# Four changes of order in a four-layer graph network kernel: the gather of layer 0, the first y2T, the aggregate and the last output tile

## The chip, the core and the metric

The kernel runs on one core of one Trainium2 chip. The metric is the device time of one execution in microseconds (us). The core has five engines that run side by side, each taking its own instructions in order: PE (TensorE, matrix products and transposes; PEld is its loading of weights), DVE (VectorE), ACT (ScalarE), POOL (GpSimd) and SP (SyncE, which here only issues transfers, DMAs). They wait for each other through semaphores. SBUF is the working memory of 128 partitions, PSUM the smaller memory that PE writes to.

## The reference

Node features x (8 graphs of 2048 nodes with 64 features) go through four layers with one adjacency matrix A (2048 x 2048, most entries zero, each row of equal entries that sum to 1). Each layer adds its result to x and normalises over the features:

```python
x = _layernorm(x + _L0_gnn_ref(x, adj, embedding, weight, bias))   # layer 0
x = _layernorm(x + _L1_gnn_ref(x, H, adj, 64, W, W_ind, ...))      # layer 1
x = _layernorm(x + _L2_gnn_ref(x, adj, weight_self, weight_neighbor, bias))
x = _layernorm(x + _L3_gnn_ref(x, adj, W))
```

Layer 0 takes x, A x and 2 A (A x) - x, and applies to each node its own 3 x 64 x 64 weights, which are a sum over 16 matrices weighted by the node's embedding:

```python
w = jnp.einsum('nd,dkio->nkio', embedding, weight)
x_g = jnp.einsum('knm,bmc->bnkc', A_stack, x)
out = jnp.einsum('bnki,nkio->bno', x_g, w)
```

Layer 1 is a hypergraph layer. Of it only the beginning matters here: every hyperedge gets a weighted mean of its members' features, with softmax weights,

```python
h = x @ W
alpha = jax.nn.softmax(jnp.where(H.T > 0, s[:, None, :], NEG), axis=-1)
agg = jnp.einsum('ben,bnf->bef', alpha, h)
```

and everything after (gates, edge scores, the weights of the edges at a node) needs agg. Layers 2 and 3 are a product with A (layer 3: A plus the identity, scaled by degrees), a 64 x 64 projection, the sum and the normalisation.

## The kernel before

The nodes lie in 16 tiles of 128 (NT = 16, index j); a tile of features is 128 x 512 (8 graphs by 64 features). A is used as a mask of zeros and ones times one number per row, and float32 products with the mask are made in two fast passes, with the high part (hi) and the rest (lo) of the other factor.

**Before layer 0**, `first_product` (from L453) makes A x for all tiles, and the product with the mask again for tile 0 (L600).

**Layer 0** is the loop at L1786. For each tile it makes eight groups, `weigh` (L1447): a group is 12 products on PE (pp, L1457) into one of two PSUM buffers (tag "pp"), and four multiply-adds on DVE (L1468) that add them, weighted by the embedding, to the tile's result r. A group can begin on PE when DVE is through with the group two before it. The order of all other steps is written out by hand between the groups: everything in a `program_order()` block keeps, on PE, DVE, ACT and POOL, the order in which the code stands. SP is not among these engines; transfers on it are put in order by the compiler's scheduler.

After group 4 of tile j comes `visit(j)` (L1712). It works for several tiles at once: `gather(j - 2)` (L1658) adds tile j-2's weighted features to the sums of all hyperedges, aggp, with two products on PE, whose inputs are hs_hi and hs_lo; `normed(j - 1, ...)` (L1485) finishes tile j-1's normalisation and writes x1; `compare(j + 1, ...)` (L1364) checks on DVE that a half tile of A is what mask times row value gives; `product(j + 1)` (L1409) makes the second product, 32 matmuls, y2p; `mask(j + 2, ...)` (L1318) makes and stores the masks of tile j+2; `counted` and `to_features` (L1433, L1549) make small products and transposes of x1; `second_term(j + 1)` (L1424) transposes y2 on PE and subtracts x on DVE, which gives y2T, the third input of `weigh` in the next tile. Between groups, POOL makes the scaled masks ms that `compare` reads (`scaled`, L1322), sums (`summed`, L1331) and the start of the next r (`begin_sum`, L1377); after group 7, `weighted` (L1640) makes hs_hi and hs_lo.

Buffers are taken by tag: tiles of one tag and pool share its `bufs` buffers in turn, and the compiler makes the first write of a new tile wait for all uses of the one whose buffer it gets. Two lines of that matter:

```python
x1s[j] = tile("y1" if j == NT - 2 else "x1", f"x1_{j}", bufs=1)                 # L1496
lo = tile("y1" if j == NT - 2 else "x1", f"hs_lo_{j}", bufs=1)                  # L1653
```

At the start of layer 0 (L1774 to L1785) the comparisons of tile 0 run in quarters (`compare_first`, L1356), with `second_term(0)` after them. At its end `last_tile` (L1739) does the normalisation and projection of tile 15 in halves, with products of layer 1 between them (`early`), the last gathers, and rden, the reciprocal of the sum of softmax weights.

**Layer 1** begins with the list `head` (L704), a string of steps that `perform` goes through: c.agg makes agg = aggp x rden on DVE (L733), c.hexp and c.he an ELU of it on ACT and DVE, c.trhe transposes it on PE (L168), and so on to the edge scores; 0.i and 1.i are products of the industry term that fill PE in between.

**Layers 2 and 3** (L1989 on) are not in a `program_order()` block: the scheduler orders their instructions. Layer 3's loop (L2045) makes, for each tile, 32 matmuls of 512 columns (L1918), and the normalisation on DVE and ACT (L2051, L137 to L156), and sends the output from ACT's queue (L2056).

Of the kernel before, what the change touches and what calls it, by code (L numbers as in the profile page):

```python
# [19 lines left out]
P = 128  # L20
# [38 lines left out]
def r_(ap):  # L59
    return ap.bitcast(F32R)  # L60
# [3 lines left out]
def kernel(  # L64
# [58 lines left out]
    def b_view(t2):  # L123
        return t2.rearrange("p (b c) -> p b c", b=B)

    def bcast(small):
        return small.unsqueeze(2).to_broadcast([P, B, C])
# [484 lines left out]
    def layer1(  # L612
# [86 lines left out]
        def column_view(src):  # L699
# [2 lines left out]
            )[:, :, :, :, 0]  # L702

        head = (  # L704
            "1.mask 2.mask 3.mask 4.mask c.agg 0.i c.hexp c.he 0.ind c.trhe c.agg1 c.heT "
            "c.fche c.sums c.the c.nagg 1.i c.sep 1.i c.serow c.sert 1.i c.ese c.eexp c.ese2 "
            "c.dnp c.ext 1.i c.rec c.hgr c.dnp2 1.i c.late "
        )
        with tc.tile_pool(name="fa", bufs=2) as fa:
# [8 lines left out]
                for n, k in (("ftr", 1), ("fmm", 1))  # L718
            )
            with program_order():  # L720
                c = {}
                low = slice(64, P)
                sums = fa.tile([P, 2, B], F32, tag="sums", name="sums", bufs=1)
                late = own.tile([P, NT - NE, 2, B], F32, tag="b0_11", name="rest_sums")
# [1 line left out]
                def parts(dst, full):  # L726

                    nc.vector.tensor_copy(r_(dst), full)
                    nc.vector.tensor_tensor(r_(dst[low]), full[low], dst[low], ALU.subtract)

                def aggregate():
                    c["agg"] = agg = fa.tile([P, BC], F32, tag="hs", name="agg", bufs=3)
                    nc.vector.tensor_tensor(b_view(agg), b_view(aggp), bcast(rden), ALU.mult)  # L733

                def exp_edges():
                    c["he"] = fa.tile([P, BC], F32, tag="xT", name="he")
# [94 lines left out]
                def other_weights():  # L831
# [1 line left out]
                    weight_sums(c["dn2"], NE, NT)  # L833

                perform(head, dict(
                    agg=aggregate, hexp=exp_edges, he=elu_edges, trhe=turn_edges, heT=turned_edges,
                    fche=fc_edges, the=tanh_edges, sep=edge_scores, serow=score_rows, sert=turn_rows,
                    agg1=lambda: parts(agg1, c["agg"]), sums=sum_edges, nagg=negated, ese=capped,
                    eexp=exp_scores, ese2=split_scores, dnp=first_weights, ext=extension,
# [439 lines left out]
    def layer0(  # L1279
# [38 lines left out]
        def mask(j, h):  # L1318
            if (j, h) not in msk:
                msk[j, h] = mask_half(mskp, raws[j][h], j, h)  # L1320
# [382 lines left out]
        def when(j, f, *args):  # L1703
            if 0 <= j < NT:
                f(j, *args)
# [5 lines left out]
        load_x(1)  # L1711
        def visit(j):  # L1712

            when(j - 2, gather)
            if j < NT - 1:
                when(j - 1, normed, 1)
            when(j + 1, compare, 0)
            if j < NT - 1:
                when(j - 1, normed, 2)
            when(j + 1, first_terms)  # L1720
            if j + 1 < NT:
                for _ in product(j + 1):
                    pass
            when(j + 2, mask, 0)
            when(j + 2, mask, 1)
            when(j + 1, compare, 1)
            counted(j + 1, j - 2)
            when(j - 1, to_features)
            if j == NT - 2:
                for t in range(len(kept_i)):  # L1730
                    for y, kept_part in zip((y_hi, y_lo), kept_i[t]):
                        nc.sync.dma_start(y[:, t, :], kept_part)
            when(j + 1, second_term)
            if j == 2:
                nc.vector.tensor_copy(rden, dens[j - 2])
            elif j > 2:
                nc.vector.tensor_tensor(rden, rden, dens[j - 2], ALU.add)

        def last_tile():  # L1739

            last = NT - 1
            early[0](6)
            half_features(0)
            gather(last - 1)
            denp = ps_p.tile([P, 2, 2, 4 * C], F32, tag="pp", name="denp")[:, 0, 0, 0:B]
            nc.tensor.matmul(denp, mds[last - 1], es[:, last - 1, :], start=True, stop=False)
            projected(last, 0)
            half_normed(1, 0)
            half_normed(1, 1)
            copied(last, 0, "sc")  # L1750
            weights_of(last, slice(0, 4))
            copied(last, 0, "h")
            copied(last, 0, "hi")
            half_normed(1, 2)
            half_weighted(0)
            copied(last, 0, "lo")
            early[0](3)
            half_features(1)
            early[0](1)
            projected(last, 1)  # L1760
            copied(last, 1, "sc")
            weights_of(last, slice(4, 8))
            half_weighted(1)
            early[0](1)
            half_gather(0)
            nc.tensor.matmul(denp, mds[last], es[:, last, :], start=False, stop=True)
            half_gather(1)
            nc.vector.tensor_tensor(rden, rden, denp, ALU.add)
            nc.vector.tensor_scalar(rden, rden, TINY, None, op0=ALU.max)
            nc.vector.reciprocal(rden, rden)  # L1770
            for what in ("h", "hi", "lo"):
                copied(last, 1, what)

        with program_order():  # L1774
            begin_sum(0)
            load_xs(1)
            mask(1, 0)
            quarters = [scaled_first(h) for h in range(2)]
            compare_first(0, quarters[0])
            mask(1, 1)  # L1780
            compare_first(1, quarters[1])
            for h in range(2):
                summed(0, h)
            second_term(0)
            scaled(1, 0)  # L1785
            for j in range(NT):  # L1786
                when(j + 2, load_adj)
                when(j + 2, load_x)
                for g in range(8):
                    weigh(j, g)  # L1790
                    if g == 0:
                        if j == 0:
                            load_weights()
                        elif j == 2:
                            late_weights()
                        if j == NT - 1:
                            centred(j - 1, 0)
                            centred(j - 1, 1)
                    elif g == 1:
                        if j < NT - 1:  # L1800
                            when(j - 1, centred, 0)
                        if j:
                            when(j + 1, scaled, 1)
                            when(j + 1, first_sum)
                    elif g == 2 and j == NT - 1:
                        normed(j - 1, 1)
                    elif g == 2 and j == 0:
                        counted(0, -1)
                        scaled(1, 1)
                    elif g == 2:  # L1810
                        centred(j - 1, 1)
                    elif g == 3 and j == NT - 1:
                        normed(j - 1, 2)
                    elif g == 3 and j:
                        next(flags, None)
                    elif g == 4:
                        visit(j)
                        if j == NT - 1:
                            spread()
                    elif g == 5:  # L1820
                        when(j + 2, scaled, 0)
                        when(j + 1, begin_sum)
                        when(j + 2, load_xs)
                        when(j - 1, project, 0)
                        if j == NT - 1:
                            half_normed(0, 0)
                            early.extend(industry_early())
                    elif g == 6:
                        if j == NT - 1:
                            half_normed(0, 1)  # L1830
                            project(j - 1, 1)
                            weights_of(j - 1)
                            weighted(j - 1)
                    elif g == 7 and j < NT - 1:
                        if j == 0:
                            score_weights(box[:, 0:2 * C].rearrange("p (i c) -> p i c", i=2))
                        when(j - 1, project, 1)
                        when(j - 1, weights_of)
                        when(j - 1, weighted)
                    elif g == 7:  # L1840
                        half_normed(0, 2)
            last_tile()
            early.pop(0)


    def short_program(top):
# [142 lines left out]
        with tc.tile_pool(name="mj2", bufs=3) as mjp, tc.tile_pool(  # L1989
# [40 lines left out]
            for j in range(NT):  # L2030
# [11 lines left out]
                if j:  # L2042
                    projected(j - 1)
            projected(NT - 1)
            for j in range(NT):  # L2045
                a = mask_tile(mjp, j, "l3")
                acc = ps_acc.tile([P, BC], F32, tag="acc", name=f"a3_{j}")
                for mt in range(NT):
                    times_mask(acc, a, v_hi, v_lo, mt)
                r = l2p.tile([P, BC], F32, tag="r", name=f"r3_{j}")  # L2050
                nc.vector.scalar_tensor_tensor(  # L2051
                    r, acc, cols_of["sdinv"][:, j:j + 1], x2[:, j, :], op0=ALU.mult, op1=ALU.add
                )
                o = l2p.tile([P, BC], F32, tag="o", name=f"o_{j}")
                layernorm(ln, r, o, f"l3_{j}")
                nc.scalar.dma_start(out[j * P:(j + 1) * P, :], o)  # L2056
# [608 lines left out]
```

## Time and profile before

| | us |
|---|---|
| median of 3 runs | 1230.51 |
| lowest and highest | 1228.17, 1231.52 |
| the profiled execution | 1229.4 |
| its span, first to last instruction | 1227.7 |
| mean granted clock of PE | 0.995 of full speed |

By stage, from the stage view of the trace (busy us of each engine):

| stretch, us | what | PE | DVE | ACT | POOL |
|---|---|---|---|---|---|
| 140 to 165 | start of layer 0 | 21.73 | 18.58 | 1.43 | 22.69 |
| 165 to 650 | layer 0 | 480.28 | 397.83 | 119.20 | 238.34 |
| 650 to 662 | its last tile | 11.91 | 8.88 | 4.61 | 4.90 |
| 662 to 680 | head of layer 1 | 15.66 | 8.91 | 4.56 | 0.07 |
| 680 to 965 | layer 1 | 269.75 | 251.81 | 196.37 | 218.34 |
| 965 to 1227 | layers 2 and 3 | 252.72 | 149.59 | 40.60 | 14.80 |

A line of a timeline reads: start in us, duration in us, engine, line of the code, operation, what is written <- what is read, shapes, count (neighbouring equal instructions are merged and counted; the duration is then that of all), and in brackets how long the engine sat idle before it and whom it waited for. Ends of matmuls are modelled.

### The profile page before, as it was taken

The numbers are of one execution on the slowest core, as the hardware profiler recorded it, in microseconds if no ns is written. First come the engines' busy times: TensorE is split into PE (matmuls) and PEld (weight loads), VectorE is DVE, ScalarE is ACT, GpSimd is POOL, SyncE is SP. The second block draws the span as 40 slices with busy tenths as digits, with TensorE's granted clock in tenths as the row PEclk, the third lists the DMA queues.
The fourth block names the chain that finished last, engine by engine and source line by source line (L and its number), as shares of the span: only waits on it lengthen the run. The fifth ranks groups of instructions, "written<-read, shape, count | busy, mean of one in ns | idle before, by whom it ended". The sixth has DMA issues, their size and how long they took to land.

```text
span 1227.7 us, 19772 instructions
## 1 busy us (share of the span) xinstructions
PE 1187.7 (97%) x7470; PEld 942.0 (77%) x7470; DVE 911.2 (74%) x1671; ACT 388.8 (32%) x1019; POOL 512.4 (42%) x429
## 2 busy tenths in 40 slices
PE   9999899999999999999999999999999999999996
PEld 7777788888888888888886655555557788888885
DVE  4555678888888888888876899988996766665454
ACT  3100102222222222222223667676676411111111
POOL 2000472555555555555511788888881700000000
PEclk9999999999999999999998999999999999999998
DMA  8977943333333333332384113122320333334541
GB/s 282 251 230 222 189 131 104 109 105 113 109 103 107 114 115 114 106 99 99 106 309 147 43 61 110 62 103 104 95 69 2 138 132 109 118 123 163 180 172 71
DMA packets 101848, 157.10 MB, mean 128 GB/s; under 512 B 13041, under 2 KB 64369, under 8 KB 96113
## 3 DMA queue, kind: packets, MB, share of 16 engines
q1 hardware_dynamic: 96944, 151.38, 38.4%
q10 hardware_dynamic: 4368, 4.33, 1.0%
q8 instruction: 61, 1.00, 0.4%
q0 software_dynamic: 432, 0.05, 0.1%
q14 instruction: 43, 0.34, 0.1%
HBM read 117.97 MB, written 37.76 MB: 127 GB/s over the span
## 4 chain that ended last, share of the span: by engine, by line
PE 73%; DVE 13%; DMA 4%; issue 3%; ACT 3%; POOL 2%; SPq 0%; DVEq 0%; ACTq 0%; POOLq 0%
PE pp L1457 26%; PE a L1918 19%; PE y2p L1414 9%; PE y1p L569 5%; PE ind L1918 3%; DMA xraw<-in_xn 2%; DVE d L947 2%; DVE ez L966 1%; DVE gp L944 1%; PE u L1146 1%; DMA adj<-in_at 1%; PE yp L2017 1%; PE try L168 1%; DVE r L1086 1%; PE hp L1582 1%
## 5 line engine op out<-in xcount | busy, mean ns | idle before, releaser
L1468 DVE SCALAR_TENSOR_TENSOR r<-pp,emb_sb,r 128x256 f32<-128x256 f32 x512 | 247.4, 483 | 78.1 <-PE pp L1457 63.9
L1457 PE MATMUL pp<-w_sb,xT 64*128 64x256 f32 x1024 | 155.4, 380 | 0.6 <-DVE r L1468 0.6
L1457 PE MATMUL pp<-w_sb,y2T 64*128 64x256 f32 x1024 | 153.5, 376 | 2.4 <-DVE y2T L1430 2.4
L1457 PE MATMUL pp<-w_sb,y1T 64*128 64x256 f32 x1024 | 153.3, 376 | 0.0
L1326 POOL TENSOR_TENSOR ms<-msk,srow 128x1024 f32<-128x1024 f32 x30 | 76.5, 2552 | 93.8 <-DVE msk L449 93.8
L1457 PEld LDWEIGHTS pp<-w_sb,y2T 64*128 64x128 f32 x1024 | 99.3, 187 | 14.0 <-DVE y2T L1430 2.8
L1457 PEld LDWEIGHTS pp<-w_sb,y1T 64*128 64x128 f32 x1024 | 99.4, 187 | 11.2
L1457 PEld LDWEIGHTS pp<-w_sb,xT 64*128 64x128 f32 x1024 | 95.1, 187 | 12.9 <-issue 2.8
L569 PE MATMUL y1p<-x_hi,m 128*128 128x512 f32 x256 | 103.0, 402 | 1.1 <-DVE y_lo L584 1.1
L569 PE MATMUL y1p<-x_lo,m 128*128 128x512 f32 x256 | 100.5, 393 | 0.0
L1918 PE MATMUL a<-v_hi,mj_l 128*128 128x512 f32 x256 | 100.1, 392 | 0.0
L1918 PE MATMUL a<-v_lo,mj_l 128*128 128x512 f32 x256 | 100.0, 391 | 0.0
L1918 PE MATMUL a<-y_lo,mj_l 128*128 128x512 f32 x240 | 95.1, 396 | 0.0
L1918 PE MATMUL a<-y_hi,mj_l 128*128 128x512 f32 x240 | 94.9, 396 | 0.0
L1414 PE MATMUL y2p<-y_hi,msk 128*128 128x512 f32 x240 | 94.7, 395 | 0.0
L1414 PE MATMUL y2p<-y_lo,msk 128*128 128x512 f32 x240 | 93.5, 390 | 0.0
L1918 PE MATMUL ind<-y_hi,mj_l 128*128 128x512 f32 x208 | 91.2, 438 | 0.1
L1918 PE MATMUL ind<-y_lo,mj_l 128*128 128x512 f32 x208 | 81.9, 394 | 0.0
L971 POOL TENSOR_TENSOR ez<-ez,coef 128x1024 f32<-128x1024 f32 x32 | 65.2, 2039 | 12.8 <-DVE ez L966 12.7
L1366 DVE SCALAR_TENSOR_TENSOR ms<-ms,adj 128x1024 f32<-128x1024 f32 x30 | 67.3, 2242 | 0.0
L1649 POOL TENSOR_TENSOR hs<-h,es 128x512 f32<-128x512 f32 x15 | 15.6, 1042 | 116.1 <-ACT hgr L1621 116.1
L925 POOL TENSOR_TENSOR d<-h,sig 128x1024 f32<-128x1024 f32 (+1 forms) x32 | 50.1, 1569 | 32.6 <-ACT sig L903 18.3
(335 smaller groups left out, 2448.8 us busy)
## 6 DMA issues: line engine op xcount, KB each, us to landing
mj_l<-mask SPq DMA_DIRECT2D x44, 1024.0 KB, 5.0
adj<-in_at SPq DMA_DIRECT2D x64, 256.0 KB, 3.8
mask<-msk SPq DMA_DIRECT2D x32, 512.0 KB, 4.5
raw<-in_at SPq DMA_DIRECT2D x31, 512.0 KB, 5.8
oh<-oh SPq DMA_DIRECT2D x32, 128.0 KB, 4.1
xT<-in_xt SPq DMA_DIRECT2D x16, 256.0 KB, 3.2
xs<-in_xn SPq DMA_DIRECT2D x16, 256.0 KB, 2.7
kept<-x SPq DMA_DIRECT2D x16, 256.0 KB, 3.4
```

The costliest lines, as they stand in the source:

```text
L168: nc.tensor.matmul(dst, src, ident, start=True, stop=True, is_transpose=True)
L569: nc.tensor.matmul(accs[q][jj], r_(m[:, t, jj * P:(jj + 1) * P]), r_(part[:, mt, :]), start=i + h + t == 0 and part is x_hi, stop=i == 3 a ...
L925: nc.gpsimd.tensor_tensor(d[:, 0:n].rearrange("p u (b c) -> p u b c", b=B), b_view(h_sb[:, j, :]).unsqueeze(1).to_broadcast([P, n, B, C]), ...
L947: nc.vector.tensor_tensor(ds[i], ds[i], gps[i], ALU.add)
L971: nc.gpsimd.tensor_tensor(by_b(ezs[i]), by_b(ezs[i]), per_b(t["coef"], 2 * i, 2), ALU.mult)
L1326: nc.gpsimd.tensor_tensor(ms, m, srow[j].unsqueeze(1).to_broadcast([P, 8, P]), ALU.mult)
L1366: nc.vector.scalar_tensor_tensor(ms, ms, 1.0, raws[j][h], op0=ALU.mult, op1=ALU.not_equal, accum_out=bad[:, 2 * j + h:2 * j + h + 1],)
L1414: nc.tensor.matmul(acc, r_(msk[j, mt // 8][:, mt % 8, :]), r_(part[:, mt, :]), start=mt == 0 and part is y_hi, stop=mt == NT - 1 and part ...
L1457: nc.tensor.matmul(pp[:, h, pl, :], terms[j][name][rs, 2 * bq + pl], w_sb[rs, k, dq * 4 * C:(dq + 1) * 4 * C], start=k == 0, stop=k == K - 1,)
L1468: nc.vector.scalar_tensor_tensor(rb, ppv[:, :, dd, :], emb_sb[:, j, d:d + 1], rb, op0=ALU.mult, op1=ALU.add)
L1649: nc.gpsimd.tensor_tensor(b_view(hs), b_view(h_sb[:, j, :]), bcast(es[:, j, :]), ALU.mult)
L1918: nc.tensor.matmul(acc, r_(a[:, mt, :]), r_(part[:, mt, :]), start=mt == 0 and part is hi, stop=mt == NT - 1 and part is lo,)
```

## The change

Four edits.

- `gather(j - 2)` in `visit` moves from the first place to behind `product(j + 1)`.
- At the start of layer 0, `second_term(0)` moves ahead of `compare_first(1, ...)` and of the POOL sums of tile 0.
- agg is made in `last_tile`, right behind rden's reciprocal and ahead of the copies of tile 15's last parts, instead of in the head of layer 1; it lies in the buffer b0_1 of `own` instead of one of the pool "fa".
- The last tile of layer 3 is made as two halves of 256 columns: 32 matmuls for each half (into PSUM buffers of two pools), then a normalisation on that half, and an output transfer each, the first issued from SP and the second from ACT.

```diff
@@ -702,7 +702,7 @@
             )[:, :, :, :, 0]
 
         head = (
-            "1.mask 2.mask 3.mask 4.mask c.agg 0.i c.hexp c.he 0.ind c.trhe c.agg1 c.heT "
+            "1.mask 2.mask 3.mask 4.mask 0.i c.hexp c.he 0.ind c.trhe c.agg1 c.heT "
             "c.fche c.sums c.the c.nagg 1.i c.sep 1.i c.serow c.sert 1.i c.ese c.eexp c.ese2 "
             "c.dnp c.ext 1.i c.rec c.hgr c.dnp2 1.i c.late "
         )
@@ -718,7 +718,7 @@
                 for n, k in (("ftr", 1), ("fmm", 1))
             )
             with program_order():
-                c = {}
+                c = {"agg": early[2]}
                 low = slice(64, P)
                 sums = fa.tile([P, 2, B], F32, tag="sums", name="sums", bufs=1)
                 late = own.tile([P, NT - NE, 2, B], F32, tag="b0_11", name="rest_sums")
@@ -727,10 +727,6 @@
 
                     nc.vector.tensor_copy(r_(dst), full)
                     nc.vector.tensor_tensor(r_(dst[low]), full[low], dst[low], ALU.subtract)
-
-                def aggregate():
-                    c["agg"] = agg = fa.tile([P, BC], F32, tag="hs", name="agg", bufs=3)
-                    nc.vector.tensor_tensor(b_view(agg), b_view(aggp), bcast(rden), ALU.mult)
 
                 def exp_edges():
                     c["he"] = fa.tile([P, BC], F32, tag="xT", name="he")
@@ -833,7 +829,7 @@
                     weight_sums(c["dn2"], NE, NT)
 
                 perform(head, dict(
-                    agg=aggregate, hexp=exp_edges, he=elu_edges, trhe=turn_edges, heT=turned_edges,
+                    hexp=exp_edges, he=elu_edges, trhe=turn_edges, heT=turned_edges,
                     fche=fc_edges, the=tanh_edges, sep=edge_scores, serow=score_rows, sert=turn_rows,
                     agg1=lambda: parts(agg1, c["agg"]), sums=sum_edges, nagg=negated, ese=capped,
                     eexp=exp_scores, ese2=split_scores, dnp=first_weights, ext=extension,
@@ -1711,7 +1707,6 @@
         load_x(1)
         def visit(j):
 
-            when(j - 2, gather)
             if j < NT - 1:
                 when(j - 1, normed, 1)
             when(j + 1, compare, 0)
@@ -1721,6 +1716,7 @@
             if j + 1 < NT:
                 for _ in product(j + 1):
                     pass
+            when(j - 2, gather)
             when(j + 2, mask, 0)
             when(j + 2, mask, 1)
             when(j + 1, compare, 1)
@@ -1768,6 +1764,9 @@
             nc.vector.tensor_tensor(rden, rden, denp, ALU.add)
             nc.vector.tensor_scalar(rden, rden, TINY, None, op0=ALU.max)
             nc.vector.reciprocal(rden, rden)
+            agg = own.tile([P, BC], F32, tag="b0_1", name="agg")
+            nc.vector.tensor_tensor(b_view(agg), b_view(aggp), bcast(rden), ALU.mult)
+            early.append(agg)
             for what in ("h", "hi", "lo"):
                 copied(last, 1, what)
 
@@ -1778,10 +1777,10 @@
             quarters = [scaled_first(h) for h in range(2)]
             compare_first(0, quarters[0])
             mask(1, 1)
+            second_term(0)
             compare_first(1, quarters[1])
             for h in range(2):
                 summed(0, h)
-            second_term(0)
             scaled(1, 0)
             for j in range(NT):
                 when(j + 2, load_adj)
@@ -2042,8 +2041,52 @@
                 if j:
                     projected(j - 1)
             projected(NT - 1)
+            def last_half(k, a):
+                j, hb = NT - 1, B // 2
+                cols = slice(k * BC // 2, (k + 1) * BC // 2)
+                pool, tag = ((ps_acc, "acc"), (ps_mm, "mm"))[k]
+                acc = pool.tile([P, BC], F32, tag=tag, name=f"a3_{j}_{k}")[:, 0:BC // 2]
+                for mt in range(NT):
+                    for part in (v_hi, v_lo):
+                        nc.tensor.matmul(
+                            acc, r_(a[:, mt, :]), r_(part[:, mt, cols]),
+                            start=mt == 0 and part is v_hi, stop=mt == NT - 1 and part is v_lo,
+                        )
+                r, sq, o = (
+                    l2p.tile([P, hb, C], F32, tag=n, name=f"{n}3_{j}_{k}") for n in ("r", "sq", "o")
+                )
+                s, var, std, rstd = (
+                    l2p.tile([P, hb], F32, tag=n, name=f"{n}3_{j}_{k}")
+                    for n in ("s", "var", "std", "rstd")
+                )
+
+                def spread(v):
+                    return v.unsqueeze(2).to_broadcast([P, hb, C])
+
+                def flat(v):
+                    return v.rearrange("p b c -> p (b c)")
+
+                nc.vector.scalar_tensor_tensor(
+                    flat(r), acc, cols_of["sdinv"][:, j:j + 1], x2[:, j, cols],
+                    op0=ALU.mult, op1=ALU.add,
+                )
+                nc.vector.tensor_reduce(s, r, AX.X, ALU.add)
+                nc.vector.scalar_tensor_tensor(
+                    r, spread(s), -1.0 / C, r, op0=ALU.mult, op1=ALU.add
+                )
+                nc.scalar.activation(flat(sq), flat(r), AF.Square, scale=C ** -0.5)
+                nc.vector.tensor_reduce(var, sq, AX.X, ALU.add)
+                nc.scalar.activation(std, var, AF.Sqrt, bias=eps_t)
+                nc.vector.reciprocal(rstd, std)
+                nc.vector.tensor_tensor(o, r, spread(rstd), ALU.mult)
+                (nc.sync, nc.scalar)[k].dma_start(out[j * P:(j + 1) * P, cols], flat(o))
+
             for j in range(NT):
                 a = mask_tile(mjp, j, "l3")
+                if j == NT - 1:
+                    for k in range(2):
+                        last_half(k, a)
+                    break
                 acc = ps_acc.tile([P, BC], F32, tag="acc", name=f"a3_{j}")
                 for mt in range(NT):
                     times_mask(acc, a, v_hi, v_lo, mt)
```

## The prediction

> **What bounds the kernel now.** I read the shares of busy time first, then the chain that ended last, then the timelines of the four places that the change touches.
>
> ```profile
> PE 1187.7 (97%) x7470; PEld 942.0 (77%) x7470; DVE 911.2 (74%) x1671; ACT 388.8 (32%) x1019; POOL 512.4 (42%) x429
> ...
> PE 73%; DVE 13%; DMA 4%; issue 3%; ACT 3%; POOL 2%; SPq 0%; DVEq 0%; ACTq 0%; POOLq 0%
> ```
>
> PE is busy 97%, and the chain is PE for 73%. In layer 0 (165 to 650 us) the stage view has PE at 480.28 of 485.00 us. So no edit there can gain by giving PE less waiting, except at its start; anything that makes PE wait is lost outright. DVE has 397.83 of the same 485, some 5.5 us of slack in each tile of 31.8 us. Here is one visit, that of tile 6 (gather of tile 4, product of tile 7, x1 of tile 5):
>
> ```profile
> 352.89 0.50 PE L1662 MATMUL aggp<-hs_hi,md 128*128 128x512 f32 x1
> ...
> 357.06 0.76 DVE L1502 TENSOR_TENSOR x<-r,rstd_l 128x256 f32<-128x256 f32 x2
> ...
> 357.74 1.29 DVE L449 TENSOR_SCALAR msk<-adj 128x1024 fp32r<-128x1024 f32 x2
> ...
> 358.51 2.77 POOL L1326 TENSOR_TENSOR ms<-msk,srow 128x1024 f32<-128x1024 f32 x1 [6.42 <-DVE msk L449]
> ...
> 358.94 3.42 DVE L1366 SCALAR_TENSOR_TENSOR ms<-ms,adj 128x1024 f32<-128x1024 f32 x1
> ...
> 360.95 0.39 PE L1414 MATMUL y2p<-y_lo,msk 128*128 128x512 f32 x1
> ...
> 361.43 0.63 PE L168 MATMUL trx<-ident,x 128*128 128x128 f32 x4
> ...
> 362.99 0.69 DVE L1430 TENSOR_TENSOR y2T<-try,xT 128x512 f32<-128x512 f32 x1 [0.62 <-PE try L168]
> ```
>
> The gather runs without waiting for its inputs (over the whole run it waited 0.2 us for POOL, once), and x1 is written 4 us before the product ends. What matters is not in these lines: hs_lo of tile j-2 and x1 of tile j-1 are both taken under tag "x1" with bufs=1 (L1653, L1496). They share one buffer. x1 may be written only after the gather has read hs_lo.
>
> **What the Trainium skill says.** "TensorE: Matmul & The Clock Gate", Architectural detail: ScalarE and VectorE queues are strict FIFO. The trace agrees: L1366, L449 and L1430 stand in program order in every visit looked at; so a DVE instruction that waits holds up all behind it. "SBUF — State Buffer", SBUF: two separate sides: a DVE operation with two SBUF inputs and a GpSimd operation exclude each other for a whole instruction. The trace agrees: L1366 takes 1.22 us alone and 3.42 beside POOL's ms above. "TensorE", LDWEIGHTS: about columns/1.2 ns, 107 ns for 128 columns; the trace has float32r matmuls of 128 columns every 0.113 us (L1401) and of 512 every 0.226, so the load is a floor that a long matmul hides.
>
> **Part 1, the gather behind the product.** It removes and adds no work: two matmuls, 0.58 us (352.89 to 353.47), move behind 32 matmuls. Product and gather together end where the product ends now, 360.95 + 0.39 = 361.34. x1 then starts at 361.39 instead of 357.06, a new DVE wait of 4.3 us. Behind it on DVE are both masks of tile j+2, the second comparison, y2T, the sum into rden and the STT (the four L1468 multiply-adds) of group 5. POOL waits for the masks, PE for x1 (trx), SP for x1 and the masks. On PE: trx can use the first half of x1, so its third transpose goes at 362.14 instead of 361.73, 0.4 late. On DVE, start to start: x1 0.68, masks 1.20, comparison 3.36 + 0.08 (ms starts after the first mask, so the clash comes along), y2T 0.61, rden 0.15, STT 2.04: 8.12 us. So STT of group 5 ends at 361.39 + 8.12 = 369.5. Group 7 needs its PSUM buffer (pp has two), and began at 368.61:
>
> ```profile
> 365.79 2.04 DVE L1468 SCALAR_TENSOR_TENSOR r<-pp,emb_sb,r 128x256 f32<-128x256 f32 x4 [1.47 <-PE pp L1457]
> ...
> 368.61 0.60 PE L1457 MATMUL pp<-w_sb,xT 64*128 64x256 f32 x4
> ```
>
> 0.9 us late; the 0.4 of trx lies inside it. STT of groups 6 and 7 then wait for PE again (as now, 0.60 and 0.55), so nothing is carried into the next tile. The edit acts where j-2 >= 0 and j+1 < 16: j = 2 to 14, 13 visits, **+11.7 us**. Bounds: the trace doesn't show this wait. Below: if the comparison escapes POOL, DVE's chain is 2.2 shorter and only 0.4 stays, +5; a gain is excluded apart from the issue gap of 0.33 that stands before the gather, which the next matmuls would probably pay. Above: if it also loses to the next POOL sum (1.28), 2.2 per visit, +28. SP: the store of x1 (358.22) moves to 362, mask stores (358.88) to 364, the next adj load (366.65) to about 371, landing in 3.8; the masks that need it run after 389. POOL: ms moves from 358.5 to 362.9, but the queue idles 8 us before hs (374.45). Both are hidden; without that cover each would cost its 4 us.
>
> **Part 2, y2T of tile 0 ahead of two comparisons.**
>
> ```profile
> 145.23 1.75 DVE L449 TENSOR_SCALAR msk<-adj 128x1024 fp32r<-128x1024 f32 x1
> 146.90 1.75 DVE L1359 SCALAR_TENSOR_TENSOR msq<-msq,adj 128x512 f32<-128x512 f32 x1
> ...
> 149.71 0.68 DVE L1430 TENSOR_TENSOR y2T<-try,xT 128x512 f32<-128x512 f32 x1
> ...
> 150.44 0.70 PE L1457 MATMUL pp<-w_sb,y2T 64*128 64x256 f32 x4 [2.44 <-DVE y2T L1430]
> ```
>
> y2T can go at 147.0, when its transposes end, and its matmuls at 147.83 instead of 150.44: -2.6. The comparisons (2.9 us) then end at 150.5, where STT of group 0 could start at 149.9; 152.5 frees the buffer that group 2 wants at 152.25: +0.3. **-2.3 us**, kept by a PE that is full from there on. Bounds -2.6 and -1.0 (POOL holding the late comparisons longer).
>
> **Part 3, the aggregate ahead of the last parts.**
>
> ```profile
> 661.23 0.49 DVE L1608 TENSOR_TENSOR y_lo<-hp,y_hi 128x128 fp32r<-128x128 f32 x2
> 661.64 0.68 DVE L733 TENSOR_TENSOR agg<-aggp,rden 128x512 f32<-128x512 f32 x1
> ...
> 664.13 0.63 PE L168 MATMUL trhe<-ident,he 128*128 128x128 f32 x4 [1.63 <-issue]
> ```
>
> The gather's last matmul ends about 661.13 (660.43 + 0.70) and rden at 661.03, so agg starts at 661.15, and exp, elu and transposes follow 0.5 earlier; PE idles 1.63 before them. y_lo comes 0.7 later; the last early product that reads it slips 0.2, inside that idle time. **-0.5 us**. Bounds 0 and -2: this stage (662 to 680) has a granted clock of 0.81, and less idle PE might keep it up.
>
> **Part 4, the last tile in two parts.** Now the last matmul ends at 1217.99 (1217.60 + 0.39), the output's DMA goes out at 1222.99, 5.0 later:
>
> ```profile
> 1218.02 0.75 DVE L2051 SCALAR_TENSOR_TENSOR r<-a,sdinv,x 128x512 f32<-128x512 f32 x1 [2.37 <-PE a L1918]
> ...
> 1222.99 0.34 ACTq L2056 DMA_DIRECT2D out<-o  x1
> ```
>
> On half the columns the steps are 0.48, 0.41, 0.42, 0.42, 0.41, 0.30, 0.20, 0.42 (L1468, L1524, L1525, L1529, L1531, L153, L154, L1502), 3.06 + 0.36 of hand-overs = 3.4, a gain of 1.6. Against it: 64 matmuls at an estimated 0.115 for 32 at 0.226, +0.1; and tile 14's normalisation (5.0 us) still fills DVE when the first half (ready at 3.7) comes, so that the first half ends near 8.0 and the second (ready at 7.4) starts 0.6 late. The transfer is half as big; "DMA: Bandwidth & Descriptors", Anatomy of one DMA, gives 436 GB/s beyond a fixed cost, an estimated 0.3 less for 128 KB, of the 2.1 that the trace shows; I take 0.1. **-1.0 us**. Bounds: -1.7 without the collision, and +1.4 if a 256-column matmul lies on the line between 0.113 and 0.226 (0.151 each, +2.4).
>
> **Sum:** 11.7 - 2.3 - 0.5 - 1.0 = +7.9. The profiled run took 1229.4 us (span 1227.7 and 1.7 around it): 1237.3. It lies 1.1 under the median of the three runs, 1230.5, which gives 1238.4; I say **1238**.
>
> **Rivals.** *The backlog grows* (slower): the comparison meets two POOL sums, 13 x 2.2 = 28.6, less 3.8: 1229.4 + 24.8 = 1254. For it: POOL's ms and sums follow each other without a gap; against: in the present run the comparison gets in after ms. *DVE's slack takes it all* (no change): only trx is late, 13 x 0.4 = 5.2 less 3.8: 1231. For it: 5.5 us of slack; against: the slack lies before group 5 to 7 only in part. *The edit is free* (faster): x1 does not wait for the moved gather, because the buffers of hs_lo and x1 turn out not to collide in time or place. Place: L1502 in each visit. Then the sum is -3.8, and -0.33 x 13 = -4.3 more if the issue gap goes: 1226 down to 1221. It decides below 0.3 us a visit (13 x 0.3 = 3.9). For it: both carry names of different tiles; against: one tag, one buffer, and DVE is in order.
>
> **Chances.** Forecast 0.56 (1232 to 1246), backlog 0.14, slack 0.14, free 0.16. Within 0.3% (about 3.7 us, what a measurement can tell from no change) holds the slack case and a little of the forecast's low end. Faster 0.17, same 0.16, slower 0.67. Range: from the free case's upper end, 1226, to the backlog's lower part, 1252.
>
> **What would show it.** Right: L1502 idle for PE aggp L1662 some 4 us in 13 visits; product starts 32.7 us apart instead of 31.8; y2T of tile 0 near 147 and no 2.44 wait; trhe half a microsecond earlier relative to the last gather; two output DMAs. Wrong: products 31.8 apart, or x1 still written during the product.

## The result, and the profile after

| us | before | after |
|---|---|---|
| median, 6 runs each | 1231.01 | 1243.86 |
| lowest to highest | 1225.84 to 1235.98 | 1243.47 to 1246.80 |
| the profiled execution, its span | 1229.4, 1227.7 | 1243.55, 1241.3 |
| mean granted clock of PE in it | 0.995 | 0.997 |

The ratio is 1.011, with a 95% interval from 1.0081 to 1.0139. The changed kernel is slower by some 13 us; the prediction had 1238 with a range of 1226 to 1252. Ratios, here and below, are of fast runs alone (within 1.5% of the fastest of the same kernel), medians of all runs.

Lines of the code have moved by four: x1 is written at L1498 (before: L1502), the comparison is L1362, y2T L1426, the multiply-adds of a group L1464, pp L1453, the gather's products L1658 (before: L1662). The busy shares of the changed kernel, from the page:

```profile
PE 1190.5 (96%) x7502; PEld 952.0 (77%) x7502; DVE 908.1 (73%) x1677; ACT 392.2 (32%) x1021; POOL 513.5 (41%) x429
```

PE does nearly the same work as before (1187.7 us), in 13.6 us more: it waits more. The view of PE's own waits, first lines (whom it waited for, us in all, times, longest):

```profile
PE hp L1578 <- DVE y2T L1426: 14.7, 12, 1.2
PE trx L168 <- DVE x L1498: 5.6, 13, 0.4
PE gp L932 <- DVE ez L962: 3.7, 8, 1.0
```

The first two are new. Before, layer 0 had another line instead, which has shrunk to 1.2 us, 2 times:

```profile
PE try L168 <- ACT deg L1445: 4.2, 15, 0.8
```

The view of all waits has the cause, as forecast:

```profile
DVE x L1498 <- PE dgp L1433: 51.7, 12, 4.4
```

(dgp is the small product right behind the gather; the trace names the last PE work that x1 waited out. There is a 13th such wait, of 4.4 us, in the last visit; the view puts it down to a DMA.) The timeline of tile 6's visit, PE and DVE:

```profile
364.42 0.39 PE L1658 MATMUL aggp<-hs_lo,md 128*128 128x512 f32 x1
...
365.48 0.68 PE L168 MATMUL trx<-ident,x 128*128 128x128 f32 x4 [0.43 <-DVE x L1498]
366.00 0.60 PE L168 MATMUL try<-ident,y 128*128 128x128 f32 x4
369.22 0.38 PE L1578 MATMUL hp<-wb,xT 64*128 64x130 f32 x2
370.83 0.60 PE L1578 MATMUL hp<-wb,xT 64*128 64x130 f32 x5 [1.22 <-DVE y2T L1426]
```

```profile
364.91 0.76 DVE L1498 TENSOR_TENSOR x<-r,rstd_l 128x256 f32<-128x256 f32 x2 [4.40 <-PE dgp L1433]
365.58 1.29 DVE L449 TENSOR_SCALAR msk<-adj 128x1024 fp32r<-128x1024 f32 x2
366.79 3.38 DVE L1362 SCALAR_TENSOR_TENSOR ms<-ms,adj 128x1024 f32<-128x1024 f32 x1
...
370.09 0.68 DVE L1426 TENSOR_TENSOR y2T<-try,xT 128x512 f32<-128x512 f32 x1
370.70 0.62 DVE L1733 TENSOR_TENSOR rden<-rden,den 128x8 f32<-128x8 f32 x1
371.24 2.03 DVE L1464 SCALAR_TENSOR_TENSOR r<-pp,emb_sb,r 128x256 f32<-128x256 f32 x4
```

x1 comes after the gather, and DVE is late in order, as the prediction had it. But PE doesn't run on to group 7. It stops after group 5, at hp, the projection of tile j-1. hp takes two PSUM buffers of tag "tr"; the second of them holds try2 until DVE's y2T has read it. The product into that second buffer starts at 370.83, 0.06 us after y2T's end (370.09 + 0.68). From the fourth of the 16 products on, the starts stand 33.62 us apart, not 31.81 (in both kernels one interval is 0.6 longer): 1.81 us in each of 12 intervals, 21.7 us. In the last visit, the 13th, x1 has no masks behind it and the comparison takes 1.22 us; there PE loses 0.65 us.

Parts 2 to 4 in the changed kernel: y2T of tile 0 goes at 145.97 and PE doesn't wait for it; agg starts 0.73 us behind the start of the last gather's last two products (678.65) instead of 1.21; the last tile's transfers are issued from both queues:

```profile
679.04 0.20 DVE L1766 RECIPROCAL rden<-rden 128x8 f32<-128x8 f32 x1
679.38 0.69 DVE L1768 TENSOR_TENSOR agg<-aggp,rden 128x512 f32<-128x512 f32 x1
...
681.89 0.63 PE L168 MATMUL trhe<-ident,he 128*128 128x128 f32 x4 [0.86 <-PE ind L1677]
```

```profile
1232.88 0.43 DVE L2081 TENSOR_TENSOR o<-r,rstd 128x256 f32<-128x256 f32 x1
1232.93 0.28 PE L2051 MATMUL a<-v_lo,mj_l 128*128 128x256 f32 x1
1233.25 0.48 DVE L2069 SCALAR_TENSOR_TENSOR r<-a,sdinv,x 128x256 f32<-128x256 f32 x1
1233.37 0.34 SPq L2082 DMA_DIRECT2D out<-o  x1
...
1236.64 0.34 ACTq L2082 DMA_DIRECT2D out<-o  x1
```

### The profile page after: what moved, and what is told of

Read it like the earlier page. It is cut to its first block, busy times and chain, and to the rows that moved or that the text cites. A ratio compares the mean times of both kernels' runs of the same rounds, so it can differ in the third digit from the quotient of the medians.

```text
span 1241.3 us, 19878 instructions
## 1 busy us (share of the span) xinstructions
PE 1190.5 (96%) x7502; PEld 952.0 (77%) x7502; DVE 908.1 (73%) x1677; ACT 392.2 (32%) x1021; POOL 513.5 (41%) x429
## 5 line engine op out<-in xcount | busy, mean ns | idle before, releaser
L1464 DVE SCALAR_TENSOR_TENSOR r<-pp,emb_sb,r 128x256 f32<-128x256 f32 x512 | 247.4, 483 | 55.9 <-PE pp L1453 41.8
L1453 PE MATMUL pp<-w_sb,xT 64*128 64x256 f32 x1024 | 180.2, 381 | 0.6 <-DVE r L1464 0.6
L1453 PE MATMUL pp<-w_sb,y2T 64*128 64x256 f32 x1024 | 177.2, 376 | 0.0
L1453 PE MATMUL pp<-w_sb,y1T 64*128 64x256 f32 x1024 | 177.1, 376 | 0.0
L1453 PEld LDWEIGHTS pp<-w_sb,y2T 64*128 64x128 f32 x1024 | 121.2, 187 | 9.7 <-DVE y2T L1426 0.2
L1453 PEld LDWEIGHTS pp<-w_sb,y1T 64*128 64x128 f32 x1024 | 121.2, 187 | 8.6
L1453 PEld LDWEIGHTS pp<-w_sb,xT 64*128 64x128 f32 x1024 | 115.7, 187 | 11.8 <-issue 2.8
L1917 PE MATMUL a<-v_hi,mj_l 128*128 128x512 f32 x240 | 93.9, 392 | 0.0
L1917 PE MATMUL a<-v_lo,mj_l 128*128 128x512 f32 x240 | 93.7, 391 | 0.0
L1362 DVE SCALAR_TENSOR_TENSOR ms<-ms,adj 128x1024 f32<-128x1024 f32 x30 | 65.7, 2190 | 0.0
L1917 PEld LDWEIGHTS ind<-y_hi,mj_l 128*128 128x128 f32 x208 | 39.4, 189 | 25.4 <-issue 16.0
```

The costliest lines, as they stand in the source:

```text
L1362: nc.vector.scalar_tensor_tensor(ms, ms, 1.0, raws[j][h], op0=ALU.mult, op1=ALU.not_equal, accum_out=bad[:, 2 * j + h:2 * j + h + 1],)
L1453: nc.tensor.matmul(pp[:, h, pl, :], terms[j][name][rs, 2 * bq + pl], w_sb[rs, k, dq * 4 * C:(dq + 1) * 4 * C], start=k == 0, stop=k == K - 1,)
L1464: nc.vector.scalar_tensor_tensor(rb, ppv[:, :, dd, :], emb_sb[:, j, d:d + 1], rb, op0=ALU.mult, op1=ALU.add)
L1917: nc.tensor.matmul(acc, r_(a[:, mt, :]), r_(part[:, mt, :]), start=mt == 0 and part is hi, stop=mt == NT - 1 and part is lo,)
```

## The experiments

Ten kernels ran, each against the kernel before on the same chip, whose median was 1230.3 to 1231.1 in these runs (27 to 75 runs). My theory after the result: part 1 costs 1.81 us a visit because x1 shares its buffer with hs_lo, and the loss is set by which DVE step the next PE instruction needs.

**e1, the gather back in first place.**

```diff
+            when(j - 2, gather)
             if j < NT - 1:
...
-            when(j - 2, gather)
             when(j + 2, mask, 0)
```

> The changed kernel with the gather put back into first place of each visit; parts 2 to 4 of the change stay. My theory now: the moved gather costs 1.81 us in each of 12 visits and the other three parts bring 2.6, 0.5 to 3 and 1.3 us. Then products stand 31.8 us apart again and the time is 1223 to 1226, 18 to 21 below the changed kernel. Rival: the cost comes from parts 2 to 4 (a longer clock spell, or the order around tile 0) or from the build as a whole; then it stays at 1236 or above and the products stand at more than 32.5.

1224.40 us, ratio 0.9946 (0.9914 to 0.9978); products 31.8 apart. Parts 2 to 4 together gain (the interval excludes 1); the whole loss is part 1.

**e2, part 1 alone** (the opposite move in the kernel before).

> The kernel before with the gather behind the product and nothing else. My theory now: 12 visits of 1.81 us, 1251 to 1254, products 33.6 us apart, DVE's x1 waiting about 4.4 us in each visit, and the projection's hp waiting about 1.2 us for y2T. The step of my forecast (0.9 us in each of 13 visits): 1241 to 1244, products 32.7 apart. Rival, the parts help each other: the parts don't add, and the time differs from 1252 by over 3 us.

1252.64 us, ratio 1.0173 (1.0121 to 1.0226); products 33.62 apart, and the same two waits (14.7 and 5.6 us). The size that I had forecast, 0.9 us a visit, is out. The parts add: +1.7% here and -0.5% for e1 make the +1.1% of the whole.

**e3, hs and hs_lo exchange buffers.** x1 then shares with hs, whose last use lies long before.

```diff
-            hs = tile("hsf", f"hs_{j}")
+            hs = tile("y1" if j == NT - 2 else "x1", f"hs_{j}", bufs=1)
...
-            lo = tile("y1" if j == NT - 2 else "x1", f"hs_lo_{j}", bufs=1)
+            lo = tile("hsf", f"hs_lo_{j}")
```

> The changed kernel, gather behind the product, with the buffers of hs and hs_lo exchanged: hs (dead after the subtraction) takes the buffer that x1 uses, hs_lo takes the one that hs had. Nothing else moves. My theory (the shared buffer is the whole cause: x1 waits for the gather to have read hs_lo): the 4.4 us wait of x1 is gone, hp doesn't wait for y2T, products stand 31.8 us apart or a little less, 1222 to 1226. Rival (the place of the gather in PE's order costs by itself: its two matmuls now stand between the product and the degree, trx and try2, and push these and with them y2T): x1's wait is gone, but products stay at 32.5 or more and the time is 1233 or above.

1218.89 us, ratio 0.9897 (0.9868 to 0.9927), the fastest of all; products 31.35 apart. Neither hp nor trx stands in PE's waits any more. It came out 3 us below what I had expected, because the moved gather does not just cost nothing. It pays. PE in e3, around the end of the product:

```profile
356.80 0.39 PE L1658 MATMUL aggp<-hs_hi,md 128*128 128x512 f32 x1
357.03 0.39 PE L1658 MATMUL aggp<-hs_lo,md 128*128 128x512 f32 x1
357.26 0.17 PE L1433 MATMUL dgp<-ones_r,both 128*128 128x2 f32 x1
...
357.51 0.64 PE L168 MATMUL trx<-ident,x 128*128 128x128 f32 x4
357.98 0.65 PE L168 MATMUL try<-ident,y 128*128 128x128 f32 x4
```

The same place before:

```profile
361.44 0.69 ACT L1420 ACTIVATE y<-y2p,s 128x512 f32<-128x512 f32 x1 [4.91 <-PE dgp L1437]
...
362.29 0.66 PE L168 MATMUL try<-ident,y 128*128 128x128 f32 x4 [0.23 <-ACT deg L1445]
```

There try2 waited 0.23 us in each visit, since ACT first had to copy y2 after the product. The gather's 0.46 us now lie in front of it, and the wait is gone.

**e6, the exchange alone,** in the kernel before, as a control.

> A control: the kernel before, gather in first place, with only the buffers of hs and hs_lo exchanged as in the fastest kernel so far. If the exchange does nothing but take the wait away that the moved gather makes, it changes nothing here: products 31.8 apart, 1228 to 1233. Rival: the exchange brings something by itself (then part of what the kernel with its own buffer gained isn't the gather's): under 1227, products below 31.7 apart.

1230.78 us, ratio 1.0006 (0.9988 to 1.0025); products 31.83 apart. The exchange brings nothing by itself, so what e3 gains over e1, 0.46 us a visit, is the gather's place.

**e4, the comparison behind y2T.**

```diff
             when(j + 2, mask, 1)
-            when(j + 1, compare, 1)
...
             when(j + 1, second_term)
+            when(j + 1, compare, 1)
```

> The changed kernel with the second comparison moved behind y2T on DVE (the masks stay in front). x1 still waits for the gather. My theory (PE stops at hp, which takes the PSUM buffer that try2 holds until y2T has read it, and then at group 7's pp, which takes a buffer that the next sum on DVE must free): y2T is done 3.4 us earlier, hp no longer waits; the sums of groups 5 on are as late as before, since the comparison still lies ahead of them, and PE stops 0.9 to 1.2 us at pp instead: products 32.7 to 33.1 apart, 1232 to 1237. Rival A (the wait at hp is the whole loss): 31.8 apart, 1222 to 1226. Rival B (hp is not what holds PE; the sums are): 33.6 apart, 1242 to 1245.

1239.24 us, ratio 1.0075 (1.0053 to 1.0098); products 33.19 apart: just outside what I had expected, and far from both rivals. (The profiled run, 1247.6, lies 8.3 us above the median. It has a wait of 8.4 us in layer 2, which of the other traces only that of e6 has; the last section comes back to it.) PE's waits in e4, the lines of layer 0:

```profile
PE pp L1453 <- DVE r L1464: 12.4, 13, 1.0
...
PE trx L168 <- DVE x L1498: 5.6, 13, 0.4
```

hp no longer waits, and group 7's pp waits for the sum of group 5 instead, the place that the prediction had named. Both rivals fall: the wait at hp is not the whole loss (31.8 apart), nor is it nothing (33.6).

**e7, hp behind group 6,** with the comparison where the change has it.

```diff
                     elif g == 5:
...
-                        when(j - 1, project, 0)
                         if j == NT - 1:
+                            project(j - 1, 0)
...
                     elif g == 6:
...
+                        else:
+                            when(j - 1, project, 0)
```

> The changed kernel with the first projection of tile j-1 moved from behind group 5 to behind group 6 (not for the last tile); comparisons and gather stay. Tells apart what the early place of hp costs from what the late sum of group 5 costs. My theory: hp no longer waits for y2T, but group 7's pp then waits for the sum of group 5, as my forecast had it: its end at 16.4 us after the product's start against group 7's earliest start at 15.0 (without hp ahead of it) to 15.4; so 33.0 to 33.6 apart, 1237 to 1244, little better than the changed kernel. Rival (hp's early place is all of the loss): 32.3 apart or less, 1229 or less.

1241.04 us, ratio 1.0123 (1.0082 to 1.0165); products 33.19 apart. The same wait as in e4, by another way: PE's early stop at hp is worth only 33.62 - 33.19 = 0.43 us.

```profile
364.75 0.76 DVE L1498 TENSOR_TENSOR x<-r,rstd_l 128x256 f32<-128x256 f32 x2 [4.42 <-PE dgp L1433]
...
370.54 0.62 DVE L1733 TENSOR_TENSOR rden<-rden,den 128x8 f32<-128x8 f32 x1
...
373.26 0.70 PE L1453 MATMUL pp<-w_sb,xT 64*128 64x256 f32 x4 [0.99 <-DVE r L1464]
```

**e5, the comparison behind the sum of group 5.**

```diff
-            when(j + 1, compare, 1)
...
                     elif g == 5:
+                        when(j + 1, compare, 1)
                         when(j + 2, scaled, 0)
```

> The changed kernel with the second comparison moved further back, behind the sum of group 5. x1 still waits for the gather. After e4, my theory is that PE's loss is set by which DVE step a PE instruction needs next: hp needs y2T's buffer, group 7 needs the sum of group 5, trx needs x1. With the comparison behind both, only the late x1 is left: products 31.9 to 32.3 apart (31.35 of the kernel with its own buffer, plus 0.6 for trx), 1224 to 1229. Rival: DVE's queue is too full to take the 4.4 us at all, the wait moves on to the sum of group 6 and so to group 0 of the next tile: 33.0 or more apart, 1238 or more.

1224.84 us, ratio 0.9969 (0.9944 to 0.9994); products 31.93 apart. x1 still waits 4.4 us in the visits. Of PE's new waits only trx's is left. DVE takes the rest, with its slack in the groups behind; the comparison is also cheaper there, since POOL's ms is over (1.33 us instead of 3.38):

```profile
358.58 0.76 DVE L1498 TENSOR_TENSOR x<-r,rstd_l 128x256 f32<-128x256 f32 x2 [4.42 <-PE dgp L1433]
...
360.47 0.68 DVE L1426 TENSOR_TENSOR y2T<-try,xT 128x512 f32<-128x512 f32 x1
...
365.08 1.33 DVE L1362 SCALAR_TENSOR_TENSOR ms<-ms,adj 128x1024 f32<-128x1024 f32 x1
```

These traces together give PE's account of one visit, from one product's start to the next (us):

| stretch | before | e3 | e5 | e4 and e7 | after |
|---|---|---|---|---|---|
| product (then gather, where moved) to trx | 7.61 | 8.07 | 8.65 | 8.66 | 8.64 |
| trx to group 5's first pp | 1.45 | 1.05 | 1.05 | 1.05 | 1.05 |
| group 5 to the next tile's group 4, with hp | 21.82 | 21.82 | 21.82 | 23.07 | 23.52 |
| rest (gather, where not moved; try1) | 0.93 | 0.41 | 0.41 | 0.41 | 0.41 |
| sum | 31.81 | 31.35 | 31.93 | 33.19 | 33.62 |

Read from left to right: the new order itself, -0.46. x1 late at trx, +0.58 (0.43 of it shown as a wait; the rest is that trx, where it need not wait, starts 0.15 us before the modelled end of the dgp ahead of it, as in e3). The sum of group 5 late at group 7, +1.26. PE stopped at hp already, ahead of group 6, +0.43.

**p2, p3, p4, the other parts alone.** Each is its part of the diff in the kernel before.

> The kernel before with y2T of tile 0 ahead of the two comparisons and nothing else. My forecast of the part: 2.3 us, kept to the end, because PE is full behind it; the first product of the loop starts some 24 us after the last one ahead of the loop instead of 26.1, and 1228 stands for the time. Rival: later work takes it back, the interval between later starts grows by as much, and the time is 1230.5. With runs that spread over 10 us, the starts in the trace tell the two apart better than the median.

1226.04 us, ratio 0.9973 (0.9942 to 1.0004): the times alone can't tell the gain from nothing, the starts can. From the last product ahead of the loop to the first in it: 24.23 us. Over all traces this interval is 25.29 to 28.95 in the five kernels without part 2 (mean 27.4), 23.49 to 24.65 in the seven with it (mean 24.0): 3.4 us. It is more than the wait. The granted clock (the share of its full clock that PE was given) by stretches, of p4, which lacks part 2, and of p2; a line gives the stretch, its length, PE's busy time and products, the clock, DMA share and GB/s:

```profile
147.00:150.00 3.00, 0.01 (x2) 1.00 0.42 118
150.00:152.00 2.00, 1.58 (x8) 0.63 0.85 274
152.00:154.00 2.00, 2.00 (x14) 0.52 0.92 311
154.00:156.00 2.00, 2.00 (x22) 1.00 1.08 293
```

```profile
147.00:150.00 3.00, 2.47 (x24) 1.00 0.37 101
150.00:152.00 2.00, 2.00 (x22) 1.00 0.74 256
152.00:154.00 2.00, 2.00 (x22) 1.00 0.88 262
154.00:156.00 2.00, 2.00 (x19) 1.00 0.79 277
```

Where y2T made PE wait 2.83, 3.40 and 3.56 us (e6, p4, p3), the clock record has 0.50 for 3.41 us, beginning between 0.5 us before and 1.2 us after the end of the wait; at 2.44 us (before), 1.60 (e2) and less it has no such spell. The interval less its wait is 25.1 to 25.4 in those three and 23.7 in the two: the spell costs 1.4 to 1.7 us on top. The Trainium skill, "TensorE: Matmul & The Clock Gate", Part 1: The HAM clock gate, gives half the clock after an idle window of about 3.4 us, windows that run free of the kernel; the half and the length of the spell agree, the wait that sufficed here was shorter. What wait suffices is not settled by these traces: in the head of layer 1 ten of the twelve have spells at 0.50 too, of 3.41, 6.83 or 10.24 us, and no single wait of PE there is above 1.63 us.

> The kernel before with the aggregate ahead of tile 15's last parts and nothing else. My forecast of the part: 0.5 us, in the dependency alone; agg starts 0.73 behind the last gather instead of 1.21, and the turning of the edges 3.24 instead of 3.70. Rival (it also shortens the spell of a low clock, as the trace of the changed kernel seemed to show, 3 us in all): the first use of the gates comes 16 to 17 us behind the last gather instead of 18.4, more than 1 us beyond the dependency. If the spell is a matter of the run and not of the edit, this distance may come out anywhere between 15.4 and 18, whatever the edit.

1228.59 us, ratio 0.9985 (0.9955 to 1.0015). The times can't show half a microsecond; the starts can: agg is 0.74 behind the last gather and trhe 3.25; in all twelve traces these are 1.20 to 1.21 and 3.69 to 3.71 without part 3, 0.73 to 0.74 and 3.24 to 3.25 with it. From the last gather to the gates: 15.8 to 18.4 without it (five traces, mean 17.1), 15.4 to 17.8 with it (seven, mean 16.6). The two ranges overlap, and the spell of a low clock there comes with and without the edit; so the rival is not borne out, and only the half microsecond is shown to be the edit's.

> The kernel before with the last tile of layer 3 in two parts and nothing else. From the trace of the changed kernel: the last output transfer is issued about 11.1 us after the last product of tile 14 instead of 12.3, a gain of 1.26, made of 1.6 for the half-sized normalisation, less 0.44 for 64 products of 256 columns that take 0.120 us each, and with no collision of the two halves. My forecast of the part was 1.0. Rival: the second transfer's own queue or landing takes it back, and the tail behind the issue grows above 4.7.

1231.75 us, ratio 0.9986 (0.9955 to 1.0016), which can't tell 1.3 us from nothing. In the trace, from the start of the last product to the issue of the last transfer: 3.71 us instead of 5.39, -1.68; the 64 products of 256 columns take 64 x 0.120 = 7.68 us instead of 32 x 0.226 = 7.23, +0.45. Net -1.23, as in the changed kernel.

## Why the prediction was right or wrong

**Part 1, mechanism: right.** The shared buffer holds x1 back by 4.4 us (forecast 4.3) in 12 of the 13 visits and by 3.2 in one; DVE's order carries it on; e3 takes the sharing away and the loss is gone, and e6 shows that the exchange of buffers brings nothing else. "DVE's slack takes it all" and "the backlog grows" did not happen: PE waits at hp in 12 visits, and the comparison took 3.38 us (forecast 3.36), beside one POOL operation.

**Part 1, size: wrong, at the step "Group 7 needs its PSUM buffer ... 0.9 us late".** It is 1.81. Two things were missed. First (0.43 of the missing 0.91), the step took group 7 for the first PE instruction that needs late DVE work. I had followed the buffers of tag "pp" and not those of tag "tr": hp stands between groups 5 and 6 on PE, and takes the buffer that y2T frees. Second (0.48), even at group 7 the delay is larger: e7, where besides trx only that stop is left, stands 33.19 - 31.81 = 1.38 above the kernel before. There x1 starts at 364.75 and group 7 at 373.26, 8.51 later, where I had 8.12. This 0.39 is rden, 0.54 from start to start instead of 0.15; the last 0.1 was not traced. 0.155 was the shortest of its 13 in the trace of before; their median was 0.70, which idle time behind it hid. A POOL operation runs beside it, and rden ends 0.02 to 0.03 us behind that one's end in every visit where it is long (in the changed kernel the sum ends at 371.29 and rden at 371.32; in e4 rden so took 1.22, in e5 1.72). The Trainium skill, "SBUF — State Buffer", Terms, has DVE and GpSimd lock a shared port pair for a whole instruction, and the loser wait; I had applied it to the large comparison and not to the eight-column add behind it. That the 0.4 of trx lies inside the later stop was right. In all 1.81 x 12 = 21.7 us, and 0.65 in the 13th visit, for 11.7 forecast.

**The free rival, faster.** It lost because of the buffer, and e3 is what it described: 1218.9, where it gave 1226 down to 1221 with 2.3 us less from the other parts. Its -0.33 a visit was measured at -0.46, mostly for another reason: the issue gap does go, but the matmuls behind pay it back but for 0.06, as the prediction thought likely, and 0.40 lies between trx and group 5, where try2 had waited for ACT. This also answers the prediction's opening: with PE busy 480 of 485 us it saw nothing to gain in layer 0 from less waiting, yet there was this much. The busy time counts modelled ends, so it hides a part of such pieces.

**Part 2: right in sign, too small.** -2.3 was forecast; the changed kernel's own trace has -2.65, the mean over traces -3.4. The forecast took the wait of 2.44 us from one run. In the five kernels without part 2 the wait is 1.60 to 3.56 us: y2T stands at 148.8 to 149.7, behind masks that wait for a transfer, while PE has its transposes at 144.9 to 146.4. A long wait brings the half clock too.

**Part 3: right,** -0.46 by dependency for -0.5. The trace of the changed kernel alone would have misled: there the head of layer 1 and what follows it was 3 us shorter, of which p3 and the other traces leave the half microsecond.

**Part 4: right,** -1.23 for -1.0, by wrong terms. I had a collision of the halves (+0.6): the scheduler let the first half's sum into a gap of tile 14's normalisation, and its output is begun at 1232.88, before the second half needs DVE at 1233.25. I had the products at +0.1: 0.120 us for 256 columns, near my lower bound of 0.113, makes +0.45. The section that the prediction cites for the smaller transfer is about transfers issued by GpSimd (POOL), while these go out from SP and ACT. The halves landed 1.71 and 2.22 us after their issue, the transfers of the full size before 2.1 in the median; no run here shows the estimated 0.3.

**The sum.** +7.9 forecast, +14.2 between the profiled runs (1229.4 and 1243.55). Part 1 alone was mis-sized by 10 us; parts 2 to 4 brought 6.1 (e1 against before) instead of 3.8. That the total still lies in the range is in part luck: the two misses pull in opposite directions.

## What to carry to other kernels

When an instruction is moved later, list everything that its inputs' buffers are reused for; a tag with one buffer is an order between two steps that no line of code shows, and exchanging a long-lived tile with a short-lived one of the same size (e3) can remove it for nothing. When an engine in order falls behind, go through each instruction of the bounding engine from there on, with each of its buffers, and ask which late step it needs. Follow the buffers of every tag, and price each stop by itself, for they hide each other: without the stop at hp, the next one, at group 7, still cost 1.26 of the 1.70 us behind trx. If the delay can't be removed, move what nobody waits for (here a comparison) behind what somebody does: e5 has the same late x1 as the changed kernel, and its median is 19 us lower.

## What the runs showed of the hardware that was not expected

- An eight-column add on DVE (rden) took 0.155 us at its shortest, 0.62 at the median in the changed kernel, 1.22 in e4 and 1.72 in e5; each of the longer ones, in the six traces looked at, ended 0.02 to 0.03 us behind the end of a POOL operation beside it.
- The first L140 of layer 2, a DVE operation, runs beside a row of POOL additions. In ten traces it took 0.83 to 0.87 us. In e4 and e6 it took 10.73 and 10.75, to 0.55 us behind the end of the whole row; PE waited 8.4 us, and the clock record has 0.50 for 6.83 us there. That the row holds it up is read from these ends and tested by no run. No edit touches this place; what decides between the two cases is open. The lines of e6:

```profile
968.22 10.75 DVE L140 SCALAR_TENSOR_TENSOR r<-s_l,r 128x512 f32<-128x512 f32 x1
...
982.31 1.12 PE L168 MATMUL tr_l<-ident,x 128*128 128x128 f32 x4 [8.44 <-DVE x L156]
```

- Waits of PE of 2.83 to 3.56 us cost 1.4 to 1.7 us more than themselves: with each came 3.41 us at half the clock, in three traces of three.
- float32r products (the fast passes with the mask), each with its own load of weights, follow each other every 0.120 us at 256 columns and every 0.226 at 512.
- The times of one kernel go with its mean granted clock: of 71 runs of the kernel before that entered the ratios of p2 to p4 and e5, the 16 with a clock above 0.9955 have a median of 1225.5 us, the 19 below 0.9905 of 1241.0. That the clock is the cause is not shown: a wait such as that of e6 makes both a longer time and a lower clock. Parts of 1 us are read from starts in the trace, not from medians.
